# Writing out every engine's order by hand in a convolution and attention kernel: depthwise taps, Winograd transforms, reciprocals and a spread on ScalarE's queue

## The chip, the cores and the metric

The kernel runs on one core of a Trainium2 chip. The metric is the device time of one execution in microseconds (us). A profiled execution gives the trace; its own time stands beside its span (first to last instruction) below.

## The reference, cut to what matters

The input x is (8, 512, 32, 32) in float32. Two layers follow each other, each as x + layer(groupnorm(x)) with 32 groups of 16 channels.

```python
# layer 0: C = 256, two inner blocks, 4 heads of 64
t = silu(bn(conv1x1(gn(x), cv1_w)));  ys = [t[:, :256], t[:, 256:]]
for i in range(2):
    z = silu(bn(conv3x3(ys[-1], m_cv1_w[i])))
    q, k, v = split(conv1x1(z, m_qkv_w[i]))              # 4 heads, 1024 positions
    a = softmax(q @ (k + rw + rh) / 8);  z = a @ v
    ys.append(ys[-1] + silu(bn(conv1x1(z, m_cv2_w[i]))))
x = x + silu(bn(conv1x1(concat(ys), cv2_w)))             # 1024 -> 512 channels
# layer 1
h = prune(relu(bn(depthwise3x3(gn(x)) + dw_b)), 4.0)     # a channel whose maximum is under 4 becomes 0
x = x + prune(relu(bn(conv1x1(h, pw_w) + pw_b)), 0.001)
```

## The kernel before, in words

A run of `fast_kernel` does all the work; `general_kernel`, a slow form behind a flag, is not entered on these inputs. Channels lie on the 128 partitions, so an image is `KC` = 4 chunks of [128, 1024]. The outer loop is over the `B` = 8 images. For image b the stages are:

1. `cv1` (L398): the first 1x1 convolution. Output tiles m = 2, 3 go to `yp[0]`, m = 0, 1 are four half tiles `ps_y` into `y0`.
2. `conv3(0)` (L432): the 3x3 convolution in Winograd form. `along_rows(j)` and `across_rows(j)` (VectorE, with two narrow copies on ScalarE) make the transformed inputs in the idle tiles `kr`, `vt`, `qy` for j = 0, 1, 2; `products(j)` (L505) multiplies them with weights from the ring, twice for each j (m = 0, 1); `rows_back` copies one component with ScalarE (L517) and combines four with VectorE (L520 to L523); the closing step subtracts the outer plane (L555) and applies Silu (L557) to give `z[:, m]`.
3. `qkv(0)` (L567): `ps_qk` for k (VectorE adds one bias table at L591, GpSimd the other at L594), `ps_v` (copied at L608), `ps_qk` for q (copied at L612). All use the two PSUM buffers of `ps_big`.
4. `attention` (L615): 32 steps of two halves each. `scores(s)` makes `ps_s` (L633), ScalarE takes `Exp` into `e` (L641), VectorE adds up `sum` (L648); `values(s - 2)` accumulates `ps_av` (L657). TensorE runs one `scores` and one `values` in 1.72 us. When a half's 16 steps are done, `sums(m)` multiplies the sums with ones (`ps_dn`, L676), VectorE takes the reciprocal (L683), ScalarE copies `ps_dn` for a range check (L684), eight DMAs of 64 KB spread the reciprocals over the partitions into `rw` (L690), and `scale(m)` multiplies `z[:, m]` with them (L699). For m = 0 this happens in the middle of the loop (s = 20 to 28), for m = 1 after it.
5. `cv2m(0)` (L721): four tiles `ps_m`, each a k = 0 and a k = 1 matmul (k = 1 reads `z[:, 1]`), Silu, and an add into `yp[1]`.
6. `conv3(1)`, `qkv(1)`, `attention`, `cv2m(1)`: the second block.
7. `cv2` (L739): four output tiles of eight k steps (`ps_cv`, L757); `finish(m)` (L765) applies Silu on ScalarE (L159) and adds into `xt[m]` (L770).
8. Layer 1. `layer1_front` (L333): group norm statistics of `xt` (L303, L304), small matmuls `pm` and `pv` (L310, L318), `xn` and the middle tap on ScalarE (L324, L353), eight taps a chunk on VectorE (L350), Relu on ScalarE, a maximum (L359) and the pruning product on GpSimd (L361). `layer1_back` (L369): `ps_pw` half tiles (L377), Relu, maximum (L391), add into `xt` (L393), store. Layer 1 of image b fills holes of image b + 1: its pieces are closures in lists (`front`, `late`, `back`), and `pump(list, n)` emits the next n pieces at the place where it stands.

The order in the source is not the order on the engines: the tile framework's scheduler may move an instruction ahead of others on its engine when it holds that it is ready. `tc.issue_after` in `conv3` pins one group. Loads of x, the weight ring (`NRING` = 4 tiles of 1 MB) and stores go through SP's queue, in the scheduler's order.

Of the kernel before, what the change touches and what calls it, by code (L numbers as in the profile page):

```python
# [8 lines left out]
F32 = mybir.dt.float32  # L9
# [4 lines left out]
P = 128  # L14
# [15 lines left out]

@with_exitstack
def fast_kernel(
# [16 lines left out]
    nc = tc.nc  # L49
# [283 lines left out]
    def layer1_front():  # L333

        norm = {}

        def normed(c):
            norm[c] = work_tile("xn")
            return norm[c]

        gn = [group_norm(xt, normed, chunks) for chunks in ((0, 1), (2, 3))]
        work = [gn[0][0], None, gn[0][1], None, gn[0][2], None, gn[0][3], None]
        for c in range(KC):

            def tap(t, c=c):
                dst, src = img(ht[c]), img(norm[c])
                dy, dx = t // 3 - 1, t % 3 - 1
                o = dst[:, max(0, -dy) : F - max(0, dy), max(0, -dx) : F - max(0, dx)]
                i = src[:, max(0, dy) : F - max(0, -dy), max(0, dx) : F - max(0, -dx)]
                nc.vector.scalar_tensor_tensor(o, i, dw[:, c, t : t + 1], o, ALU.mult, ALU.add)  # L350

            def first(c=c):
                nc.scalar.mul(ht[c], norm[c], dw[:, c, 4:5])  # L353

            def last(c=c):
                norm.pop(c)
                act(ht[c], ht[c], AF.Relu, BN4 + c)
                keep = small.tile([P, 1], F32, tag="keep", name="keep")
                nc.vector.tensor_reduce(keep, ht[c], AX.X, ALU.max)  # L359
                nc.vector.tensor_scalar(keep, keep, 4.0, None, ALU.is_ge)  # L360
                nc.gpsimd.tensor_scalar(ht[c], ht[c], keep, 1.0, ALU.mult, ALU.mult)  # L361

            apply = gn[c // 2][4 + c % 2]
            work.append(lambda apply=apply, first=first: (apply(), first()))
            work += [lambda t=t, tap=tap: tap(t) for t in range(9) if t != 4]
            work.append(last)
        return work, gn[1][:4]

    def layer1_back(b):  # L369
# [4 lines left out]
        def half(m, n):  # L374
# [11 lines left out]
            w = box[m]  # L386
            act(w[:, n * 512 : (n + 1) * 512], ps, AF.Relu, BN5 + m)
            if n == 0:
                return
# [6 lines left out]
        return [lambda m=m, n=n: half(m, n) for m in range(KC) for n in range(2)]  # L396

    def cv1(stats, bg, per):  # L398

        for m in (2, 3):  # L400
            ps = big_tile("ps_cv1")
            for k in range(KC):
# [8 lines left out]
                if k == 1:  # L411
                    pump(stats)
            pump(stats)
            act(inner(yp[0], m - 2), by_phase(flat(ps)), AF.Silu, BN0 + m)
            pump(bg, per)
# [14 lines left out]
        return [lambda m=m, n=n: half(m, n) for m in range(2) for n in range(2)]  # L430

    def conv3(l, fill):  # L432
# [61 lines left out]
        def products(j):  # L494
# [4 lines left out]
            with Weights() as wt:  # L499
                u = wt.rearrange("p (i c k o) -> p i c k o", i=2, c=4, k=2)  # L500
                for c in (1, 2, 0, 3):
                    for i in range(2):
                        at = place[c] * 256 + i * P
                        for k in range(2):
                            keep["ins"] = nc.tensor.matmul(  # L505
# [19 lines left out]
        across_rows(0, along_rows(0))  # L525
        across_rows(1, along_rows(1))
        inner_planes = [work_tile("mid") for _ in range(2)]
        outer_planes = [work_tile("mid") for _ in range(2)]
        for m in range(2):
            rows_back(products(0), inner_planes[m][:, :512])  # L530
        across_rows(2, along_rows(2))
        ys = []
        for m in range(2):
            rows_back(products(1), inner_planes[m][:, 512:])
# [16 lines left out]
        for m in range(2):  # L551
            pc = outer_planes[m][:, :512]
            rows_back(products(2), pc)
# [10 lines left out]
        with tc.issue_after(keep["ins"].ins):  # L564
            pump(fill, len(fill))

    def qkv(l, bg, per):  # L567
        with Weights() as wt:
# [16 lines left out]

            for m, ps in enumerate(products((2, 3))):
# [28 lines left out]
    def attention(bg, every, tail):  # L615
# [85 lines left out]
        for s in range(len(steps) + 2):  # L701
# [4 lines left out]
            if s == 20:  # L706
                check = sums(0)
# [593 lines left out]
```

## Time and profile before

| what | value |
|---|---|
| median of 3 runs | 2950.03 us (2949.51 to 2951.57) |
| the profiled execution | 2950.13 us, span 2948.3 us, mean granted TensorE clock 0.974 |
| TensorE / VectorE / ScalarE / GpSimd busy | 91% / 66% / 39% / 6% of the span |
| one steady image | 354.9 us (ps_c of conv3(0) at 764.51 us to the same at 1119.37 us) |
| TensorE busy in that image | 331.9 us |
| VectorE, ScalarE busy in that image | 235.9 us, 142.2 us |
| chain that ended last | TensorE 55%, VectorE 23%, ScalarE 5% of the span |

How to read the rows in the next part: a timeline row gives the start and length in us, the engine (a "q" after it: its queue's issuing part), the line, the operation with output and inputs, the form, a count, and in brackets the idle time before it with what ended it. A matmul in float32 appears as two records. A window row gives the stretch, then the busy time of TensorE, its weight loads, VectorE, ScalarE and GpSimd, then the granted TensorE clock and the DMA engines' share and rate. In a row for a line, three durations are the least, the median and the greatest in ns.

### The profile page before, as it was taken

What the parts mean: (1) busy time and instruction counts of PE and PEld (TensorE: products, weight loads), DVE (VectorE), ACT (ScalarE), POOL (GpSimd) and SP (SyncE); (2) the same over time, 40 slices, a digit from 0 to 9 for tenths busy, and PEclk for the clock granted to TensorE, in tenths of its full rate; (3) what the DMA queues carried; (4) which work ended last, traced back from release to release, by engine and by line L of the source; (5) the groups of instructions that cost most, each with busy time, mean ns of one, the idle gap of its engine ahead of it and who ended that gap; (6) DMA issues with size and microseconds to landing.
All of it is one profiled execution on the core that took longest, in us unless ns stands there. A gap on an engine that the chain in (4) does not pass through costs nothing.

```text
span 2948.3 us, 36194 instructions
## 1 busy us (share of the span) xinstructions
PE 2676.8 (91%) x14946; PEld 1449.8 (49%) x14946; DVE 1932.4 (66%) x2513; ACT 1160.0 (39%) x1386; POOL 163.0 (6%) x97
## 2 busy tenths in 40 slices
PE   6879989999899998999999999999989999899984
PEld 4444454544646445464454545545454544545431
DVE  6765478753976639665596646975478753877536
ACT  3534335253352533524334342434325343352522
POOL 1000001000100001000010000100001000100001
PEclk9989999999999999999999999999999999999997
DMA  8510130311303013130131202221121301203000
GB/s 322 192 61 23 57 118 30 111 30 63 113 23 125 15 65 125 30 111 15 57 126 43 97 21 78 98 86 54 43 98 63 112 29 50 97 22 118 22 7 30
DMA packets 90333, 219.75 MB, mean 75 GB/s; under 512 B 8880, under 2 KB 54192, under 8 KB 77616
## 3 DMA queue, kind: packets, MB, share of 16 engines
q1 hardware_dynamic: 89728, 216.04, 21.5%
q8 instruction: 119, 1.95, 0.3%
q10 hardware_dynamic: 432, 1.32, 0.1%
q14 instruction: 54, 0.44, 0.0%
HBM read 171.19 MB, written 29.36 MB: 68 GB/s over the span
## 4 chain that ended last, share of the span: by engine, by line
PE 55%; DVE 23%; ACT 5%; issue 2%; SPq 1%; POOL 1%; DMA 0%; DVEq 0%; ACTq 0%; POOLq 0%
PE ps_cv L757 12%; PE ps_av L657 12%; PE ps_s L633 11%; DVE ht L350 10%; PE ps_c L505 8%; PE ps_pw L377 4%; PE ps_qk L577 3%; PE ps_m L726 3%; DVE r L683 2%; PE ps_v L601 2%; ACT e L641 1%; DVE kr L591 1%; SPq L690 1%; ACT c L159 1%; DVE keep L359 1%
## 5 line engine op out<-in xcount | busy, mean ns | idle before, releaser
L633 PE MATMUL ps_s<-qy,kr 64*64 64x512 f32 x4096 | 576.2, 595 | 79.9 <-ACT e L641 78.6
L641 ACT ACTIVATE e<-ps_s 128x1024 f32<-128x1024 f32 x512 | 520.1, 1024 | 269.0 <-PE ps_s L633 266.5
L657 PE MATMUL ps_av<-e,vt 64*64 64x512 f32 x4096 | 572.2, 593 | 0.0
L648 DVE TENSOR_TENSOR sum<-sum,e 128x1024 f32<-128x1024 f32 x384 | 471.8, 1229 | 152.2 <-ACT e L641 144.7
L633 PEld LDWEIGHTS ps_s<-qy,kr 64*64 64x64 f32 x4096 | 208.7, 133 | 330.0 <-ACT e L641 132.9
L657 PEld LDWEIGHTS ps_av<-e,vt 64*64 64x64 f32 x4096 | 225.4, 133 | 222.5 <-issue 145.0
L350 DVE SCALAR_TENSOR_TENSOR ht<-xn,v_sb,ht 128x961 f32<-128x961 f32 (+1 forms) x256 | 318.1, 1283 | 5.0 <-ACT ht L353 4.4
L377 PE MATMUL ps_pw<-ht,wpw_sb 128*128 128x512 f32 x512 | 230.8, 605 | 27.1 <-POOL ht L361 27.1
L757 PE MATMUL ps_cv<-yp,wring 128*128 128x512 f32 x512 | 230.4, 596 | 0.0
L577 PE MATMUL ps_qk<-z,wring 128*128 128x512 f32 x512 | 226.7, 596 | 2.8 <-ACT z L557 2.8
L645 DVE TENSOR_TENSOR sum<-e 128x1024 f32<-128x1024 f32 x64 | 78.2, 1221 | 199.1 <-ACT e L641 196.3
L505 PE MATMUL ps_c<-kr,wring 128*128 128x128 f32 x1024 | 138.8, 305 | 57.5 <-ACT kr L492 39.9
L377 PEld LDWEIGHTS ps_pw<-ht,wpw_sb 128*128 128x128 f32 x512 | 97.1, 193 | 153.9 <-issue 112.5
L505 PEld LDWEIGHTS ps_c<-kr,wring 128*128 128x128 f32 x1024 | 136.0, 220 | 70.5 <-ACT kr L492 45.5
L517 ACT COPY c<-ps_c 128x256 f32<-128x256 f32 x96 | 35.8, 373 | 331.5 <-PE ps_c L505 281.3
L577 PEld LDWEIGHTS ps_qk<-z,wring 128*128 128x128 f32 x512 | 97.8, 191 | 119.3 <-issue 113.5
L770 DVE TENSOR_TENSOR xt<-c,xt 128x1024 f32<-128x1024 f32 x32 | 39.2, 1226 | 176.0 <-ACT c L159 176.0
L757 PEld LDWEIGHTS ps_cv<-yp,wring 128*128 128x128 f32 x512 | 95.5, 190 | 118.2 <-issue 118.2
L594 POOL TENSOR_TENSOR kr<-kr,v_sb 128x1024 f32<-128x1024 f32 x32 | 75.0, 2357 | 1298.8 <-DVE kr L591 1225.6
L159 ACT ACTIVATE c<-ps_cv,bi,sc 128x1024 f32<-128x1024 f32 x32 | 69.7, 2178 | 194.4 <-PE ps_cv L757 194.4
L683 DVE RECIPROCAL r<-ps_dn 128x512 f32<-128x512 f32 x32 | 107.3, 3354 | 49.9 <-PE ps_dn L676 49.9
L726 PE MATMUL ps_m<-z,wm_sb 128*128 128x512 f32 x256 | 119.2, 604 | 20.4 <-DVE z L699 20.4
(167 smaller groups left out, 3152.8 us busy)
## 6 DMA issues: line engine op xcount, KB each, us to landing
wring<-u SPq DMA_DIRECT2D x96, 1024.0 KB, 4.8
pt<-in_x SPq DMA_DIRECT2D x32, 512.0 KB, 5.8
xt<-in_x SPq DMA_DIRECT2D x32, 512.0 KB, 3.5
rw<-r SPq DMA_DIRECT2D x256, 64.0 KB, 2.0
wring<-in_w SPq DMA_DIRECT2D x32, 512.0 KB, 4.2
out<-xt SPq DMA_DIRECT2D x32, 512.0 KB, 2.7
wring<-in_wqkv SPq DMA_DIRECT2D x16, 768.0 KB, 4.3
u<-ucomp SPq DMA_DIRECT2D x24, 256.0 KB, 2.8
```

Of the source, the lines that this page charges most:

```text
L159: nc.scalar.activation(o, i, func, bias=bi[:, n : n + 1], scale=sc[:, n : n + 1])
L350: nc.vector.scalar_tensor_tensor(o, i, dw[:, c, t : t + 1], o, ALU.mult, ALU.add)
L377: nc.tensor.matmul(ps, wpw_sb[:, k, m * P : (m + 1) * P], ht[k][:, n * 512 : (n + 1) * 512], start=(k == 0), stop=(k == KC - 1),)
L505: keep["ins"] = nc.tensor.matmul(flat(ps)[:, at : at + P], u[:, i, c, k, :], component(j, c)[:, (2 * i + k) * P : (2 * i + k + 1) * P], st ...
L577: nc.tensor.matmul(ps[:, n, :], w[:, k, m * P : (m + 1) * P], z[:, k, n * 512 : (n + 1) * 512], start=(k == 0), stop=(k == 1),)
L633: nc.tensor.matmul(ps[half(c), a, :], kr[half(a), m, j : j + HD], qy[half(a), m, ih * 512 : (ih + 1) * 512], start=True, stop=True,)
L641: nc.scalar.activation(flat(e), flat(ps), AF.Exp, scale=HD ** -0.5)
L648: nc.vector.tensor_tensor(t, t, flat(e), ALU.add)
L657: nc.tensor.matmul(accs[m, ih][r][half(a), :], vt[half(r), jt, h * HD : (h + 1) * HD], e[half(r), a, :], start=(jt == 0), stop=(jt == last),)
L683: nc.vector.reciprocal(r[:, :512], dn)
L726: nc.tensor.matmul(ps, wm2_sb[:, l, k, m * P : (m + 1) * P], z[:, k, n * 512 : (n + 1) * 512], start=(k == 0), stop=(k == 1),)
L757: nc.tensor.matmul(ps[:, n, :], w[:, k, :], rhs(k, n), start=(k == 0), stop=(k == 2 * KC - 1),)
```

## The change

A wrapper around TensorE, VectorE, ScalarE and SP makes each instruction depend (without a semaphore) on the one that was written before it for the same engine, so that the scheduler keeps the written order. GpSimd is left as it was. The order itself is then written out: which tap, statistic, transform or finishing step stands between which others. Besides that,

- the reciprocal is split into four pieces of 128 columns, in steps 20 to 23 for m = 0 (`sums` moves from step 20 to 19, the spread is at step 25, `scale` at 29), and the check copy of `ps_dn` is written ahead of them;
- the eight DMAs that spread the reciprocals are issued from ScalarE's queue instead of SP's;
- `layer1_back` is split into half tiles and `finish(m)`; `layer1_front` gives separate lists `early`, `late`, `before`, `taps`;
- in `conv3` the row transforms for j = 2 stand ahead of the first `rows_back`, and `along_back`, `close` and the fillers have fixed places;
- the second block's weight transform for image 0 is spread over `qkv(0)` (15 pieces) instead of standing ahead of the attention.

```diff
+class InOrder:
+    def __getattr__(self, name):
+        method = getattr(self.engine, name)
+        def call(*args, **kwargs):
+            made = method(*args, **kwargs)
+            if self.last is not None:
...
+                self.tc.add_manual_dep(made.ins, self.last, how, reason="in_order")
+            self.last = made.ins.name
+            return made
+        return call
+class Engines:
...
+        self.tensor, self.vector = InOrder(tc, nc.tensor), InOrder(tc, nc.vector)
+        self.scalar, self.sync = InOrder(tc, nc.scalar), InOrder(tc, nc.sync)
+        self.gpsimd = nc.gpsimd
...
-    nc = tc.nc
+    nc = Engines(tc)
# layer1_front
+        def before(c):
+            gn[c // 2][4 + c % 2]()
+            nc.scalar.mul(ht[c], norm[c], dw[:, c, 4:5])
...
+            taps += [lambda c=c, t=t: tap(c, t) for t in range(9) if t != 4]
+            taps[-1] = lambda c=c, last=taps[-1]: (last(), relu(c))
+            if c:
+                taps.insert(9 * c, lambda c=c: prune(c - 1))
+        taps.append(lambda: prune(KC - 1))
+        return gn[0][:4], gn[1][:4], [lambda c=c: before(c) for c in range(KC)], taps
# conv3
-        with tc.issue_after(keep["ins"].ins):
-            pump(fill, len(fill))
+        across_rows(0, along_rows(0))
+        pump(fill, early)
+        across_rows(1, along_rows(1))
+        pair = along_rows(2)
+        rows_back(products(0), inner_planes[0][:, :512])
+        across_rows(2, pair)
+        rows_back(products(0), inner_planes[1][:, :512])
+        rows_back(products(1), inner_planes[0][:, 512:])
+        along_back(0)
+        rows_back(products(1), inner_planes[1][:, 512:])
+        pump(ends_work)
+        along_back(1)
+        ms = products(2)
+        pump(ends_work)
+        close(0, ms)
+        ms = products(2)
+        flush(fill)
+        close(1, ms)
+        flush(ends_work)
# sums
-            nc.vector.reciprocal(r[:, :512], dn)
             nc.scalar.activation(r[:, 512:], dn, AF.Copy, accum_out=rng[:, n : n + 1])
+            def part(q):
+                c = slice(q * 128, (q + 1) * 128)
+                nc.vector.reciprocal(r[:, c], dn[:, c])
+            def spread():
...
-                    nc.sync.dma_start(
+                        nc.scalar.dma_start(
...
+            if s == 19:
+                parts, spread, check = sums(0)
+            if 20 <= s < 24:
+                parts[s - 20]()
+            if s == 25:
+                spread()
+                check()
+            if s == 29:
                 scale(0)
-            if s % every == every - 1:
+            if s in when:
                 pump(bg)
         flush(bg)
         tail[0]()
-        check = sums(1)
+        parts, spread, check = sums(1)
+        for part in parts:
+            part()
+        spread()
         tail[1]()
         scale(1)
         check()
# the loop over images
+        first, y0_work = cv1()
+        pump(first)
+        pump(taps, 2)
+        pump(late)
+        pump(first)
+        pump(taps, 2)
+        pump(late)
+        pump(before)
+        pump(first)
+        pump(taps, 2)
+        pump(before)
+        pump(first)
+        pump(taps, 3)
+        pump(y0_work, 2)
+        conv3(0, y0_work, 1, [])
...
+            taps = transform_weights(1)
+        elif b + 1 < B:
+            load(pt, b + 1)
+        qkv(0, taps, (4, 2, 2, 2, 2, 2, 2))
+        attention(taps, QUIET, (lambda: pump(halves), lambda: pump(halves, 2)))
+        pump(finishes)
...
         cv2m(0)
+        pump(halves, 2)
+        conv3(1, halves, 1, finishes)
         load(xt, b)
+        stats = group_norm(pt, lambda c: pt[c], range(KC)) if b + 1 < B else []
+        qkv(1, [], (0,) * 7)
         products, finish = cv2()
         attention(
             stats[:KC],
+            (6, 10, 14, 17),
+            (lambda: products(0, (0, 1)), lambda: (products(0, (2, 3, 4, 5)), products(1, (0,)))),
         )
...
+        early, late, before, taps = layer1_front()
+        products(1, (1, 2, 3))
...
+        products(2, (5, 6, 7))
+        pump(before)
         finish(2)
+        pump(taps, 3)
         pump(late)
+        products(3, (0, 1, 2, 3))
+        pump(taps, 3)
+        pump(before)
+        products(3, (4, 5, 6, 7))
+        pump(taps, 4)
         finish(3)
         pump(late)
+        halves, finishes = layer1_back(b)
```

## The prediction

> **What bounds the kernel now.** I read the page's busy times first, then TensorE's timeline over one steady image (764.5 to 1119.4 us), then the ScalarE and VectorE timelines beside each hole in it, and last the window table for the granted clock.
>
> ```profile
> PE 2676.8 (91%) x14946; PEld 1449.8 (49%) x14946; DVE 1932.4 (66%) x2513; ACT 1160.0 (39%) x1386; POOL 163.0 (6%) x97
> ```
>
> TensorE is busy 91% and the change alters none of its work, so only the other 271 us and the clock can move. These timeline rows start after the holes (in brackets: idle time, and who ended it):
>
> ```profile
> 764.51 9.47 PE L505 MATMUL ps_c<-kr,wring 128*128 128x128 f32 x64 [5.71 <-ACT kr L492]
> 824.68 1.09 PE L633 MATMUL ps_s<-qy,kr 64*64 64x512 f32 x8 [2.45 <-ACT e L641]
> 860.84 1.09 PE L633 MATMUL ps_s<-qy,kr 64*64 64x512 f32 x8 [1.91 <-ACT e L641]
> 894.43 4.56 PE L726 MATMUL ps_m<-z,wm_sb 128*128 128x512 f32 x10 [1.80 <-DVE z L699]
> 919.55 7.38 PE L505 MATMUL ps_c<-vt,wring 128*128 128x128 f32 x64 [2.35 <-issue]
> 1093.21 0.38 PE L310 MATMUL pm<-mv,g_sb 128*128 128x2 f32 x2 [0.81 <-DVE mv L304]
> ```
>
> With smaller ones (.98 before ps_v, .89 in conv3(0), 1.25 at each attention start, 1.91 in the second attention) an image has 23 us of holes. A hole can cost twice. The window table's columns are us, then busy time by engine, then granted clock:
>
> ```profile
> 764.50:768.90 4.40, 4.39 (x20) 4.40 (x21) 4.37 (x8) 0.34 (x2) 1.90 (x1) 0.50 0.00 0
> 563.80:567.40 3.60, 3.60 (x18) 3.60 (x19) 3.60 (x8) 0.00 (x0) 0.00 (x0) 0.54 0.94 366
> 919.60:923.20 3.60, 3.60 (x33) 3.60 (x34) 3.58 (x8) 0.00 (x0) 0.00 (x0) 1.00 0.93 387
> ```
>
> After the 5.7 us hole the clock is halved for 4.4 us (2.2 lost); after the 2.35 us hole at 563.8 for 3.4 (1.7 lost), after the same hole at 919.6 not at all. In conv3(1) three of seven such holes did it, the 5.7 ones always, holes up to 2.46 in attention never.
>
> **The change part by part.** I followed the instruction order of the changed program on each engine; TensorE's is nearly the old one.
>
> *Taps.* Before, VectorE runs 16 taps between the last cv2 tile and conv3(0), and TensorE waits for it.
>
> ```profile
> 738.84 5.80 DVE L350 SCALAR_TENSOR_TENSOR ht<-xn,v_sb,ht 128x961 f32<-128x961 f32 x5
> ```
>
> A tap is 1.14 us. The new order puts nine during products(3), where VectorE idles 10.9 us, and eight (9.1 us) after. Counted from the end of products(2): cv1's second tile ends at 31.1 on TensorE, its Silu, behind xn and ht of chunks 2 and 3, at 33.1, relu(1) and prune(1) at 35.5, four transform steps and the first kr (.6 each) at 38.6; TensorE has three y0 halves (10.3) until 41.4. Cover 2.8: hole 5.7 to 0, half clock gone, 7.9 us on each of images 1 to 7: −55.
>
> *Its price at pm.* ScalarE now does relu(0), behind eight taps, ahead of finish(3)'s Silu. From the same start: Silu 2.2, add 1.25, three taps 3.4, statistics 1.5, five taps 5.7, relu 1.25: 15.3, against 13.8 for products(3). Silu 2.2, add 1.25 and statistics 1.5 end at 20.3; TensorE, after four cv1 matmuls (3.4), is at pm at 17.2. The hole goes from .8 to some 3.2: +2.4, seven times: +17.
>
> *conv3(0) and qkv(0).* The last y0 Silu stands ahead of close(1)'s copy: from the end of that half on TensorE, Silu .8, copy .4, four combining steps 1.35, ends .6 and Silu 1.25 bring z[1] after 4.5, and the k=0 half of qk covers 3.4: 1.1. Four taps (4.6) stand ahead of the first kr add (1.84), which so begins as qk ends; both PSUM buffers are taken and ps_v waits 1.75, then .5 for the second add behind two taps. That is 3.35 instead of 2.05: +1.4 with the clock left alone, seven times: +10. At the attention's start relu(3) stands ahead of the Exp table load (1.25 to 3.15), but the 2.45 hole from a relu among the Exps goes: −.5, −4.
>
> *conv3(1).* The finish(m) work (2.55 us each) no longer sits between VectorE's vt operations: holes .5, 2.35, .18, .34 become about 1.05 (the same late copy, here behind two pw Silus): −2.3 seven times, −16, and the three half clocks −5.
>
> *Reciprocal and spread.* Before, the .6 us copy waits for the 3.36 us reciprocal, and the Exps behind both; SP issues the eight DMAs.
>
> ```profile
> 853.54 1.02 ACT L641 ACTIVATE e<-ps_s 128x1024 f32<-128x1024 f32 x1 [0.69 <-PE ps_s L633]
> 859.19 0.60 ACT L684 ACTIVATE r<-ps_dn 128x512 f32<-128x512 f32 x1 [4.62 <-DVE r L683]
> 859.77 1.02 ACT L641 ACTIVATE e<-ps_s 128x1024 f32<-128x1024 f32 x1
> ```
>
> An Exp 4.5 us late thus left a hole of 1.9 beside 1.0 of ps_dn matmuls: 1.6 is absorbed. Quarters hide the reciprocal: one takes .84 beside a sum of 1.14, step 1.72. But the DMAs now stand in ScalarE's own queue at s=25, with check() (.72) and every later Exp behind them. Their price:
>
> ```profile
> L690 SPq DMA_DIRECT2D rw<-r x256: 507/588/1764, 156.5 to 2814.5; - x128
> DMA to landing us min/median/max: 1.9/2.0/3.8
> 0.73 0.41 ACTq L92 DMA_DIRECT2D v_sb<-in_vecs  x1
> 1.66 0.45 ACTq L96 DMA_DIRECT2D w_sb<-in_w  x1
> ```
>
> No row has this transfer on ScalarE. It lies between .43 (its three loads) and .59 (the same transfer on SP) an issue; I take .59, the row with the same shape. Eight with the gaps between them are 5.0. ScalarE idles .7 between Exps, so the next is 5.0 + .7 − .7 = 5.0 late, hole 5.0 − 1.6 = 3.4 instead of 1.9: +1.5, sixteen times: +25. At .43 the eight are 3.6 and the sum is 1.4 less each time.
>
> [...]
>
> *Attention's ends.* The new reciprocal waits for ScalarE's copy (.7, and .3 for four pieces; 512 columns take .68 and 256 .41 in the transforms, so some .1 of an instruction is fixed), so z[1] comes 12.4 us after ps_dn instead of 11.4. Written order also gives cv2m one k=0 matmul before it needs z[1], where three ran before (.86 each). cv2m(0): cover 6.9+.86, hole 4.7 instead of 1.8. cv2m(1): ten cv2 matmuls (8.6) and one, hole about 3.0 to 3.3 instead of none. Together +5.9, eight times: +47. The pw Silus queued behind the spread finish before z[1] does.
>
> *The ends.* Image 0 has the second weight transform in qkv(0) instead of ahead of attention (hole 10.7): about −3. The last image has nine taps done early, but three pw matmuls fewer: −4. The moved pt, xt and ring loads and the pt statistics cost nothing: they land in steps that TensorE fills (30 us and more of cover; uncovered, a load's landing is 3 to 6 us).
>
> *The clock.* New holes above 3 us: pm and the attention start (7 each), mid-attention (16), cv2m (8 and 8). Between three in seven (2.35 us) and always (5.7) I take .65, for the 4.7 ones .9: 32 events. At 1.5 (1.7 less what lies in the hole): +48. Bounds: 0, and 46 at 1.7, +78.
>
> [...]
>
> Sum: −55+17+10−4+25+47−16−5−7+48 = +60. The profiled execution took 2950.1 us (span 2948.3), the runs' median 2950.0, so 3010.
>
> **The rivals.**
> 1. An issue on ScalarE costs what its three loads did (.43), or the clock mostly holds. Mid-attention and cv2m lose 1.4 less in 32 places (−45), and some 15 clock events go (−22): 2943. For it: the ACTq rows. Against: other shapes, and on SP 128-row loads are cheaper (.33) than rw.
> 2. The issue costs ScalarE under .1 us. The mid-attention holes vanish (3.4 × 16 = 54), those at cv2m shrink to 1.0 and 0 (55), 23 clock events go (34): 2867, clearly faster. It decides below about .45 an issue, where the sum crosses zero. No row is below .32.
> 3. VectorE is still last at conv3(0), since taps beside GpSimd's kr adds are slower (six took 8.6 us at 804): the 55 is not won, 3065.
>
> That the order isn't kept is no rival: the built program shows it.
>
> **How the numbers follow.** The forecast gets .63, rivals .2, .08 and .09. Within .2% (about what a measurement of this kernel can tell from no change) is 2944 to 2956. The forecast's own range, clock from none to all, is 2962 to 3040: slower. Rival 1 splits: .12 faster, .05 same, .03 slower. Faster .12+.08 = .20, same .05, slower .75. The range takes in rival 1 and most of rival 3, leaving out rival 2 and some of each tail: 2922 to 3060.
>
> **What the changed profile would show.** All operations will carry the wrapper's one line, so rows go by tiles. Right: ScalarE's queue rows for rw of .55 or more in groups of eight, a hole near 3.4 before ps_s in mid-attention, 4 to 5 before ps_m in cv2m(0), about 3 in cv2m(1) and at pm, none before ps_c<-kr, and PEclk .50 stretches behind some of them. Wrong: rw issues near .1, cv2m holes under 2, a hole still before conv3(0), or these holes with the clock at 1.00.

## The result, and the profile after

The changed kernel takes 3090.43 us (median of four runs, 3087.06 to 3092.15) against 2949.77 for the kernel before: ratio 1.0474, interval 1.0456 to 1.0492. It is slower, as forecast, but by 141 us and not by 60, and outside the stated range (2922 to 3060). The profiled execution has a span of 3085.3 us against 2948.3: 137.0 to explain.

The page of the changed kernel, busy times and the chain that ended last:

```profile
PE 2745.5 (89%) x14946; PEld 1411.1 (46%) x14946; DVE 1975.7 (64%) x2609; ACT 1166.1 (38%) x1386; POOL 157.7 (5%) x97
PE 64%; DVE 21%; ACT 6%; ACTq 4%; DMA 2%; issue 2%; POOL 0%; DVEq 0%; SPq 0%; POOLq 0%
```

TensorE has the same 14,946 matmul records and is busy 68.7 us longer, while its mean granted clock fell from 0.974 to 0.951, with stretches at half clock (0.50 in the window rows below). Its idle time grew by 68.3 (span less busy). So one half of the loss is holes (idle time of TensorE), the other half clock. ScalarE's queue (ACTq), 0% of the chain before, now carries 4% of it.

TensorE's timeline, one image (770.2 to 1142.7 us, 372.5 long; 354.9 before). Each row stands behind a hole, which is in brackets with what ended it:

```profile
770.16 0.59 PE L41 MATMUL pm<-mv,g_sb 128*128 128x2 f32 x2 [4.34 <-DVE mv L41]
...
830.28 3.72 PE L41 MATMUL ps_v<-wring,z 128*128 128x256 f32 x16 [1.83 <-DVE kr L41]
836.11 1.38 PE L41 MATMUL ps_v<-wring,z 128*128 128x256 f32 x4 [2.10 <-DVE kr L41]
...
854.52 1.99 PE L41 MATMUL ps_s<-qy,kr 64*64 64x512 f32 x8 [3.95 <-ACT e L41]
...
905.63 1.13 PE L41 MATMUL ps_s<-qy,kr 64*64 64x512 f32 x4 [3.33 <-ACT e L41]
...
932.76 2.07 PE L41 MATMUL ps_m<-z,wm_sb 128*128 128x512 f32 x2 [4.35 <-DVE z L41]
...
1055.94 1.13 PE L41 MATMUL ps_s<-qy,kr 64*64 64x512 f32 x4 [4.31 <-ACT e L41]
...
1083.20 1.22 PE L41 MATMUL ps_m<-z,wm_sb 128*128 128x512 f32 x1 [2.83 <-DVE z L41]
```

The hole before `ps_c<-kr` is gone, as forecast; mid-attention and cv2m are where the forecast put them. Not forecast at this size: the two ps_v holes, the 3.95 at the attention's start, and pm's 4.34. The window table (us, busy time by engine, granted clock) behind three of these holes and behind one of the next image:

```profile
836.90:840.20 3.30, 3.30 (x9) 2.64 (x8) 3.30 (x3) 2.14 (x2) 2.11 (x1) 0.50 0.00 0
854.60:857.30 2.70, 2.70 (x16) 0.88 (x20) 1.23 (x1) 1.45 (x2) 0.00 (x0) 0.50 0.03 6
905.70:908.50 2.80, 2.80 (x16) 0.97 (x20) 2.36 (x2) 1.55 (x2) 0.00 (x0) 0.50 0.01 3
1429.40:1432.80 3.40, 3.40 (x32) 1.21 (x36) 3.19 (x3) 2.35 (x3) 0.00 (x0) 1.00 0.00 0
```

The last row is an exception (one of two among 33 holes above 3 us): a hole of 3.33 with the clock left whole. ScalarE issues rw at the price that was assumed (median .603 against .59):

```profile
L41 ACTq DMA_DIRECT2D rw<-r x256: 514/603/1389, 168.4 to 2942.4; - x128
```

Forecast and measurement by stage, cut at the first matmul of each (the first pm of an image stands in cv2), clock included, over the whole program (us):

| stages | forecast | measured |
|---|---|---|
| pm to the end of conv3(0) (taps, pm, clock) | -31 | -31 |
| qkv(0) | +10 | +56 |
| both attentions, to the first ps_m | +43 | +63 |
| cv2m(0), cv2m(1) | +66 | +60 |
| conv3(1), qkv(1) | -21 | -21 |
| start of the program and last image's end | -7 | +10 |
| sum | +60 | +137 |

Two cv2 matmuls an image (1.72 us) run in the second attention in the changed kernel and behind the first pm in the kernel before. Without this shift of work the first row is -19, the attentions +49, cv2m +63 and the ends +8.

### The profile page after: what moved, and what is told of

The parts are those of the page before. It is cut to its first block, busy times and chain, and to the rows that moved or that the text cites. A ratio compares the mean times of both kernels' runs of the same rounds, so it can differ in the third digit from the quotient of the medians.

```text
span 3085.3 us, 36329 instructions
## 1 busy us (share of the span) xinstructions
PE 2745.5 (89%) x14946; PEld 1411.1 (46%) x14946; DVE 1975.7 (64%) x2609; ACT 1166.1 (38%) x1386; POOL 157.7 (5%) x97
## 4 chain that ended last, share of the span: by engine, by line
PE 64%; DVE 21%; ACT 6%; ACTq 4%; DMA 2%; issue 2%; POOL 0%; DVEq 0%; SPq 0%; POOLq 0%
PE ps_av L41 14%; PE ps_s L41 13%; PE ps_cv L41 12%; DVE ht L41 8%; PE ps_c L41 8%; PE ps_m L41 4%; PE ps_pw L41 4%; ACTq L41 4%; PE ps_y L41 3%; PE ps_qk L41 3%; DMA rw<-r 2%; PE ps_v L41 2%; DVE r L41 2%; DVE mid L41 2%; DVE kr L41 2%
## 5 line engine op out<-in xcount | busy, mean ns | idle before, releaser
L41 PE MATMUL ps_s<-qy,kr 64*64 64x512 f32 x4096 | 579.1, 615 | 98.3 <-ACT e L41 96.8
L41 ACT ACTIVATE e<-ps_s 128x1024 f32<-128x1024 f32 x512 | 520.7, 1023 | 316.1 <-PE ps_s L41 315.9
L41 DVE TENSOR_TENSOR sum<-sum,e 128x1024 f32<-128x1024 f32 x384 | 470.6, 1225 | 208.1 <-ACT e L41 200.5
L41 PE MATMUL ps_av<-e,vt 64*64 64x512 f32 x4096 | 569.4, 607 | 0.0
L41 PEld LDWEIGHTS ps_s<-qy,kr 64*64 64x64 f32 x4096 | 191.9, 137 | 376.9 <-issue 175.3
L41 DVE SCALAR_TENSOR_TENSOR ht<-xn,v_sb,ht 128x961 f32<-128x961 f32 (+1 forms) x256 | 342.5, 1345 | 5.8
L41 PEld LDWEIGHTS ps_av<-e,vt 64*64 64x64 f32 x4096 | 201.9, 137 | 264.1 <-issue 212.7
L41 PE MATMUL ps_pw<-ht,wpw_sb 128*128 128x512 f32 x512 | 232.7, 608 | 32.6 <-POOL ht L394 32.6
L41 PE MATMUL ps_qk<-z,wring 128*128 128x512 f32 x512 | 232.5, 598 | 18.0 <-DVE mid L41 14.3
L41 PE MATMUL ps_cv<-yp,wring 128*128 128x512 f32 x512 | 231.1, 597 | 0.0
L41 DVE TENSOR_TENSOR sum<-e 128x1024 f32<-128x1024 f32 x64 | 78.4, 1225 | 228.2 <-ACT e L41 228.2
L41 PE MATMUL ps_m<-z,wm_sb 128*128 128x512 f32 x256 | 143.3, 712 | 62.1 <-DVE z L41 62.1
L41 PEld LDWEIGHTS ps_pw<-ht,wpw_sb 128*128 128x128 f32 x512 | 97.0, 194 | 161.3 <-issue 115.7
L41 PE MATMUL ps_v<-wring,z 128*128 128x256 f32 x512 | 130.5, 416 | 36.6 <-DVE kr L41 36.6
L41 PEld LDWEIGHTS ps_qk<-z,wring 128*128 128x128 f32 x512 | 94.4, 190 | 143.5 <-issue 122.1
L41 DVE RECIPROCAL r<-ps_dn 128x128 f32<-128x128 f32 x128 | 114.8, 928 | 61.4 <-ACT r L41 61.4
L41 PEld LDWEIGHTS ps_cv<-yp,wring 128*128 128x128 f32 x512 | 94.9, 190 | 114.3 <-issue 114.3
L41 PEld LDWEIGHTS ps_v<-wring,z 128*128 128x128 f32 x512 | 104.9, 209 | 69.0 <-DVE kr L41 52.9
L41 PE MATMUL ps_cv<-pt,w_sb 128*128 128x512 f32 x256 | 132.5, 674 | 2.8 <-ACT pt L41 2.8
L41 PE MATMUL ps_c<-kr,wring 128*128 128x128 f32 x1024 | 121.5, 281 | 14.8 <-DMA wring<-u 9.7
L41 PEld LDWEIGHTS ps_c<-kr,wring 128*128 128x128 f32 x1024 | 121.1, 198 | 23.1 <-ACT vt L41 10.5
```

The source lines that it names most:

```text
L41: made = method(*args, **kwargs)
```

## The experiments

All times are medians. The letter E and a number name a run; "changed" is the changed kernel at 3090. Each run carried a fresh time of the kernel before (2949.7 to 2950.9).

| run | what | us | ratio to before |
|---|---|---|---|
| E1 | changed, spread on SP | 3005.8 | 1.0192 (1.0175 to 1.0209) |
| E2 | changed, no taps between VectorE's kr adds | 3085.0 | 1.0459 (1.0442 to 1.0477) |
| E3 | changed, three items behind finish(3) | 3100.1 | 1.0505 (1.0487 to 1.0522) |
| E4 | changed, second spread on two queues | 3034.6 | 1.0283 (1.0266 to 1.0300) |
| E5 | E2, and three items into the attention | 3033.0 | 1.0278 (1.0261 to 1.0295) |
| E6 | E3's items behind pv | 3091.7 | 1.0480 (1.0462 to 1.0497) |
| E7 | before, spread on ScalarE | 3061.3 | 1.0379 (1.0361 to 1.0396) |
| E8 | changed without the wrapper | 2872.7 | 0.9733 (0.9717 to 0.9749) |
| E9 | wrapper on TensorE alone | 3039.3 | 1.0297 (1.0279 to 1.0316) |
| E10 | wrapper on ScalarE alone | 2936.9 | 0.9957 (0.9942 to 0.9972) |
| E11 | wrapper on VectorE alone | 2943.1 | 0.9974 (0.9965 to 0.9984) |
| E12 | E8, spreads on SP and on both queues | 2803.8 | 0.9505 (0.9488 to 0.9522) |
| E13 | changed, pm and pv later | 3089.4 | 1.0469 (1.0450 to 1.0488) |
| E14 | changed, three k = 0 matmuls ahead | 3043.2 | 1.0313 (1.0295 to 1.0331) |
| E15 | written order, all places mended | 2855.4 | 0.9679 (0.9662 to 0.9696) |
| E16 | E15's source (less pm, k = 0) without the wrapper | 2802.0 | 0.9495 (0.9478 to 0.9512) |
| E17 | E15, two more moves on ScalarE | 2827.8 | 0.9584 (0.9568 to 0.9600) |

### The spread: E1, E4, E7

E1, one word in `spread()`:

```diff
-                        nc.scalar.dma_start(
+                        nc.sync.dma_start(
```

> The changed kernel with the eight spreading DMAs on SP's queue again. Theory: at mid-attention it is the eight issues (5.0 us) in ScalarE's own queue that hold the next Exp; with them on SP only the check copy (.63) is left ahead of it, so the holes of 3.33 and 4.31 before ps_s fall to 0 to .5 and the half-clock windows behind them go: about 10 us an image, 75 to 80 in all, some 3010 us (2995 to 3030). The cv2m holes stay at 4.35 and 2.83, since SP issues at the same pitch (.633 before) and the order of the steps is unchanged. Rival: the mid-attention holes come from the new order around the reciprocal (copy first, four pieces, the check waiting for r); then they stay at 1.9 or more and the time falls by under 25 us.

Measured: 3005.8, 85 less than changed. The mid-attention holes are gone, cv2m keeps 4.4 and 2.6. ScalarE's timeline at mid-attention, first of the changed kernel, then of E1:

```profile
898.88 5.01 ACTq L41 DMA_DIRECT2D rw<-r  x8
903.95 0.63 ACT L41 ACTIVATE r<-r 128x512 f32<-128x512 f32 x1 [4.50 <-DMA rw<-r]
904.48 0.19 ACT L41 ACTIVATION_READ_ACCUMULATOR r<-r 128x1 f32 x1
904.57 1.92 ACT L41 ACTIVATE e<-ps_s 128x1024 f32<-128x1024 f32 x2
```

```profile
884.61 0.58 ACT L41 COPY part<-ps_av 128x512 f32<-128x512 f32 x1
885.07 0.64 ACT L41 ACTIVATE r<-r 128x512 f32<-128x512 f32 x1
885.60 0.20 ACT L41 ACTIVATION_READ_ACCUMULATOR r<-r 128x1 f32 x1
885.70 1.02 ACT L41 ACTIVATE e<-ps_s 128x1024 f32<-128x1024 f32 x1
```

Two Exps come back to back at 904.57 after 5.7 us of DMA issues and check; with the issues on SP an Exp follows the check at once.

E4 sends the second spread's DMAs alternately:

```diff
-                        nc.scalar.dma_start(
+                        q = nc.scalar if m == 0 else (nc.sync, nc.scalar)[h]
+                        q.dma_start(
```

> The changed kernel with the eight DMAs of the second half's spread (the one after the attention loop) issued in turn from SP and ScalarE, four each; the first half's stay on ScalarE. Theory: at cv2m the chain copy, four reciprocals, eight issues one after the other, landing, scale sets z[1]; two queues issue in 2.5 us instead of 5.0, so the holes 4.35 and 2.83 fall to about 1.9 and .4, and the half clocks behind them go: 2.45 + 1.7 (less where a window had fallen into the hole), twice an image, 55 to 66 us in all, some 3030 us (3020 to 3045). Rival: the landing takes longer when two queues issue at once, or one queue's issue price rises, so that the holes shrink by under 1 us: 3070 to 3090.

Measured: 3034.6, 56 less. cv2m(0) 4.35 to 2.2, cv2m(1) 2.83 to .5. ScalarE and SP, side by side:

```profile
1279.79 2.44 ACTq L41 DMA_DIRECT2D rw<-r  x4
1279.86 2.67 SPq L41 DMA_DIRECT2D rw<-r  x4
```

The two queues issue at once here, four in 2.44 and four in 2.67, where the eight on ScalarE's took 5.01; the median landing stays 2.0.

E7 puts the spread on ScalarE in the kernel before, nothing else:

> The kernel before with one change: the eight spreading DMAs issued from ScalarE's queue. Nothing else, no written order. Theory: the eight issues (5.0 us) stand ahead of the next Exps, behind the whole reciprocal, and nothing absorbs them: the mid-attention hole grows from 1.9 to about 6.9, with a half-clock window behind it (1.7 or more), 16 times: +105 us, 3055 us (3035 to 3075); the holes at cv2m stay as they are, since the issue pitch is the same. Rival: the issues overlap with the wait for the reciprocal or with VectorE's sums, and the spread is worth no more than the +25 of the forecast: 2965 to 2985.

Measured: 3061.3, 112 more than before. TensorE's hole there grew from 1.91 to 6.55:

```profile
1253.89 0.51 ACTq L690 DMA_DIRECT2D rw<-r  x1
1254.28 0.19 ACT L684 ACTIVATION_READ_ACCUMULATOR r<-ps_dn 128x1 f32 x1
1254.44 4.46 ACTq L690 DMA_DIRECT2D rw<-r  x7
1259.01 1.94 ACT L641 ACTIVATE e<-ps_s 128x1024 f32<-128x1024 f32 x2 [4.54 <-DMA rw<-r]
```

So the other queue is a loss in either order. That it is smaller in the changed kernel fits that its pieces hide the reciprocal, which no run tests by itself.

### qkv(0): E2, E5

> The changed kernel with the taps of qkv(0) counted (3, 0, 0, 4, 4, 3, 2) instead of (4, 2, 2, 2, 2, 2, 2): none between or behind the two kr adds. Theory: the two taps between the kr adds run beside GpSimd's add at 2.0 us each, not 1.14, and TensorE waits for the second kr add; without them the holes 1.83 and 2.10 before ps_v fall to about .4 each or less, the half clock behind them goes, and the last tap ends about 3 us sooner, so that the Relu ahead of the Exps no longer holds them: the hole at the attention's start falls from 3.95 to 1.25. Per image 3.1 + 1.7 and 2.7 + 1.7, seven times: 60 us, some 3030 (3015 to 3050). Rival: the taps only carry their price to a later place (the Relu in front of the Exps comes no sooner, the start hole stays near 4 or grows): 3060 to 3090.

```diff
-        qkv(0, taps, (4, 2, 2, 2, 2, 2, 2))
+        qkv(0, taps, (3, 0, 0, 4, 4, 3, 2))
```

Measured: 3085.0, 5 less: the rival. Both halves of the reason show in TensorE's timeline of E2:

```profile
1202.06 1.13 PE L41 MATMUL ps_v<-wring,z 128*128 128x256 f32 x4 [0.57 <-DVE kr L41]
...
1226.46 1.13 PE L41 MATMUL ps_s<-qy,kr 64*64 64x512 f32 x4 [7.78 <-ACT e L41]
```

The ps_v holes shrank from 3.93 to .57, and all of it came back before the Exps, which stand behind the last Relu. ScalarE, VectorE and GpSimd in E2:

```profile
1222.83 1.24 ACT L41 ACTIVATE ht<-ht,bi,sc 128x1024 f32<-128x1024 f32 x1 [5.30 <-DVE ht L41]
1224.09 1.28 ACT L41 ACT_TABLE_LOAD   x1
1203.83 7.86 DVE L41 SCALAR_TENSOR_TENSOR ht<-xn,v_sb,ht 128x992 f32<-128x992 f32 x5
1202.15 4.85 POOL L653 TENSOR_TENSOR kr<-kr,v_sb 128x1024 f32<-128x1024 f32 x2 [39.44 <-DVE kr L41]
```

The five taps behind VectorE's second add still run beside GpSimd's adds (until 1207.0) and take 7.86; so E2, and E5 below with the same counts there, take the taps out from between VectorE's two adds but not from beside GpSimd's, against what their expectations say. VectorE and GpSimd in the changed kernel show why the holes were there:

```profile
828.33 1.90 DVE L41 TENSOR_TENSOR kr<-ps_qk,v_sb 128x1024 f32<-128x1024 f32 x1
830.15 4.07 DVE L41 SCALAR_TENSOR_TENSOR ht<-xn,v_sb,ht 128x961 f32<-128x961 f32 x2
834.15 1.90 DVE L41 TENSOR_TENSOR kr<-ps_qk,v_sb 128x1024 f32<-128x1024 f32 x1
835.99 4.03 DVE L41 SCALAR_TENSOR_TENSOR ht<-xn,v_sb,ht 128x961 f32<-128x961 f32 x2
830.38 2.80 POOL L653 TENSOR_TENSOR kr<-kr,v_sb 128x1024 f32<-128x1024 f32 x1 [40.70 <-DVE kr L41]
```

The two taps between the adds take 4.07, not the forecast 2.3. One row for the four taps from 830.2 to 840.0 (least, median, greatest ns) tells how:

```profile
L41 DVE SCALAR_TENSOR_TENSOR ht<-xn,v_sb,ht x4: 1179/2018/2919, 830.2 to 837.1; 128x961 f32<-128x961 f32 x3, 128x992 f32<-128x992 f32 x1
```

In each pair the first tap (1.18 and 1.19) starts ahead of GpSimd's add; the second takes 2.8 to 2.9 and ends 1.04 after that add (830.38 + 2.80 = 833.18, and 834.22). E5 takes the same kernel and lets the attention's fixed places have the last three items:

```diff
-        qkv(0, taps, (4, 2, 2, 2, 2, 2, 2))
+        qkv(0, taps, (3, 0, 0, 4, 4, 2, 0))
```

> The changed kernel with the taps of qkv(0) counted (3, 0, 0, 4, 4, 2, 0): none beside GpSimd's kr adds, and the last two taps of chunk 3 with their Relu, as well as its pruning, in the attention's fixed places (steps 5, 8, 11). Theory: in the run that only moved the taps off the kr adds, the start hole grew to 7.8 because VectorE's remaining 12 pieces end no sooner than before and the Exps stand behind the last Relu on ScalarE. With three pieces fewer the Relu no longer stands ahead of the Exps: the start hole falls from 3.95 to 1.25, the two ps_v holes to about .6 together, and the half clocks of both places go: 3.3 + 1.7 + 2.7 + 2.2 = 9.9 an image, seven times some 70 us: 3020 us (3010 to 3040), less what the Relu costs among the Exps (0 to 1 an image). Rival: the Relu among the Exps costs a hole of its own of 2 to 4 (the kernel before had 2.45 there): 3040 to 3065.

Measured: 3033.0, 57 less than changed. ps_v .61, start 1.31, and one new hole of 1.42 where the Relu stands among the Exps: inside the expected span.

### The place of pm: E3, E6, E13

E3 and E6 move the four items ahead of `finish(3)`, keeping one there; E3 puts the other three right behind its statistics, E6 further on:

```diff
-        pump(taps, 4)
+        pump(taps, 1)
         finish(3)
         pump(late)
+        pump(taps, 3)          # E3 only; E6: counts 1, 2, 4, 5 in cv1
```

> The changed kernel with three of the four items (last tap of chunk 0 with its Relu, a tap of chunk 1, prune(0)) that stand ahead of finish(3) put behind the group norm statistics that follow it. Theory: the hole of 4.35 before pm is the Relu of chunk 0 ahead of finish(3)'s Silu on ScalarE (2.2 us) and the taps it waits for; with them behind, the hole falls to about 1.5 to 2.2, and the half-clock window there (6.8 us, some 2 net of the hole) goes in most images: 4 to 5 us, seven times, some 3058 us (3050 to 3070). Rival: VectorE then idles while it waits for the Silu and comes late to conv3(0): a new hole of 2 or 3 before ps_c<-kr, no gain (3080 to 3095).

> The changed kernel with three items less on VectorE ahead of finish(3) (as in the run before) and these three now behind the second small matmul pv, in the later places of cv1 (counts 1, 2, 4, 5 instead of 2, 2, 2, 3). Theory: the run before moved the same items, the pm hole fell to 1.67 as expected and the new hole of 1.99 before pv came from their standing ahead of the copy of pm; behind pv they hold nobody: pm hole 1.7, no pv hole, half clock there mostly gone: 4.3 an image, seven times, 3060 us (3050 to 3072). Rival: VectorE comes late at conv3(0) by the 3.4 us of the three items: a hole of 1 to 3 before ps_c<-kr, 3080 to 3095.

Measured: 3100.1 and 3091.7. In both the pm hole fell to 1.67, and nothing was won. E3 made a hole of 1.99 before pv (its three items stand ahead of the copy of pm). In E6 it came back as 2.88 before `ps_c<-vt` instead of .91 and, in six of seven images, 5.6 at the attention's start instead of 3.95: the rival in time, though not at the place that it named (`ps_c<-kr`). E13 leaves VectorE and ScalarE as written and gives TensorE four more matmuls to do ahead of pm and pv:

```diff
         pump(first)
         pump(taps, 2)
+        pump(first)
         pump(late)
+        pump(taps, 2)
         pump(first)
-        pump(taps, 2)
         pump(late)
         pump(before)
-        pump(first)
```

> The changed kernel, wrapper and all, with pm written four cv1 matmuls later on TensorE, and pv four later as well; all else in its place. Theory: TensorE's written order costs so much because it can't run the cv1 matmuls that are ready while pm waits for the statistics (the free order runs pm behind them, hole .94). With four of them ahead of it (3.4 us) the hole of 4.35 falls to about .9 and its half-clock window goes (3.4, of which some 2 outside the hole): 5 to 6 an image, seven times some 38 us: 3052 us (3045 to 3062). Rival: the second tile's Silu, and with it conv3(0), waits for what pv releases, and the hole only moves: 3075 or more.

Measured: 3089.4. TensorE's timeline:

```profile
1148.07 0.38 PE L41 MATMUL pm<-mv,g_sb 128*128 128x2 f32 x2 [0.92 <-DVE mv L41]
...
1167.11 7.38 PE L41 MATMUL ps_c<-kr,wring 128*128 128x128 f32 x64 [1.16 <-ACT kr L41]
1177.58 0.77 PE L41 MATMUL ps_c<-vt,wring 128*128 128x128 f32 x2 [3.08 <-ACT c L41]
```

The hole of 4.35 fell to .92 as expected, and 1.16 and 3.08 (instead of .91) stand in conv3(0): the rival (3075 or more). In six of seven images the hole in front of the Exps is 5.64 instead of 3.95, too. The mean granted clock of the run is 0.952, against 0.951 in the changed kernel. Three ways to shrink the pm hole, three times no gain: it was slack of TensorE in a stretch, from cv2's last tile to the first Exp, whose end other engines set. That these are ScalarE's and VectorE's written orders is argued here; E17 tests ScalarE's.

### The wrapper: E8 to E11

E8 is the changed kernel with `nc = tc.nc` for `nc = Engines(tc)`; in E9, E10 and E11 one engine alone is wrapped.

> The changed kernel without the wrapper: the same source order, but the scheduler may move instructions as in the kernel before. The spread stays on ScalarE. Theory: the loss lies in the spread and in the fixed places that were badly chosen (taps beside the kr adds, Relu ahead of the Silu, one k = 0 matmul ahead of z[1]); the scheduler undoes the latter but not the spread, so that it lands between the run with the spread on SP's queue and the changed kernel, some 3045 us (3020 to 3075). Rival: the scheduler moves the taps and the reciprocal pieces to worse places than the written ones: 3090 or more.

> The changed kernel with the wrapper on TensorE alone; ScalarE, VectorE and SP are left to the scheduler. The whole wrapper costs 3090 - 2873 = 217 us. Theory: TensorE's written order costs only the missing k = 0 matmuls at cv2m (the free order has three there and no hole at cv2m(1), stage 4.5 us shorter; cv2m(0) 1.6 shorter), eight times some 50 us: 2920 us (2900 to 2945). Rival: the TensorE order is where most of the loss lies (matmuls can't fill a hole any more): 2980 or more.

> The changed kernel with the wrapper on ScalarE alone. Theory: the holes of the stages that grew most are each released by ScalarE behind an operation that waits for something else: the Relu of chunk 0 ahead of finish(3)'s Silu (pm hole 4.35), the check copy behind the spread ahead of the Exps (1.7 more than in the free order, twice an image), the last Relu ahead of the table load and the Exps: 3 + 1.7 with the half clock, 3.4, 2 to 3: some 10 to 11 an image, 80 us: 2950 us (2920 to 2985). Rival: with VectorE free to feed it in the right order, ScalarE's written order costs little: under 2900.

> The changed kernel with the wrapper on VectorE alone. Theory: the two taps between the kr adds (qkv(0), 5.4 us an image longer than free, half clock counted) and the late last tap are VectorE's share, with some of the pm hole (ten taps ahead of the add): 7 to 9 an image, 60 us: 2930 us (2905 to 2965). The three single wrappers then add up to about the 217. Rival: it takes the orders of two engines together to make a wait (one in front of the wrong operation, the other unable to pass it), so that each alone costs under 30.

Measured: 2872.7 for E8, under every expectation: without the wrapper the same source, with its spread still on ScalarE, beats the kernel before by 2.7%. The page's busy line of E8 has TensorE at 93% of a span of 2871.1, and its idle time is 196.7 instead of 339.8:

```profile
PE 2674.4 (93%) x14946; PEld 1381.4 (48%) x14946; DVE 1917.3 (67%) x2609; ACT 1164.7 (41%) x1386; POOL 153.4 (5%) x97
```

Against E8, TensorE's order alone costs 167 (E9, where its rival held), ScalarE's 64, VectorE's 70. They add up to 301, more than the 218 of all together, so they share waits; SP's order alone was not run. E10 and E11 lie within their ranges, but not by the theories given. With ScalarE alone in written order pm's hole is 1.09, not 4.35, and the loss against E8 stands in qkv(0) (23 us), qkv(1) (15), cv2m(0) (12) and the attentions (18). With VectorE alone the largest part, 41, is conv3(1) with qkv(1), with a hole of 3.33 before the latter's first `ps_qk`, which the theory does not name. TensorE around pm, first E9, then E8:

```profile
1122.10 3.60 PE L41 MATMUL ps_cv<-pt,w_sb 128*128 128x512 f32 x8
1130.92 0.58 PE L41 MATMUL pm<-mv,g_sb 128*128 128x2 f32 x2 [5.22 <-DVE mv L336]
```

```profile
1070.71 7.89 PE L447 MATMUL ps_cv<-pt,w_sb 128*128 128x512 f32 x18
1079.54 0.38 PE L340 MATMUL pm<-mv,g_sb 128*128 128x2 f32 x2 [0.94 <-DVE mv L334]
```

In E9 four cv1 matmuls (8 records) run and then pm holds everything behind it for 5.22 us; in E8 the scheduler has moved nine ahead of it. By stages E9 loses against E8, an image: 7.2 from pm to conv3(0), 6.0 in conv3(1), 4.4 in cv2m(1) and 2.6 in cv2m(0), about 1.7 in each attention.

### Mending: E12, E14 to E17

E12 and E16 have no wrapper; the first spread goes to SP, the second alternately to both queues (E4's edit with `nc.sync` for m = 0). E14 writes three k = 0 matmuls ahead in `cv2m`. E15 puts E1, E4, E5, E13 and E14 together, with `close(1, ms)` ahead of `flush(fill)`; E17 moves on from E15:

```diff
         pump(taps, 2)
-        pump(before)
         pump(first)
         pump(taps, 3)
+        pump(before)
...
+        if l:
+            flush(fill)
         close(1, ms)
         flush(fill)
```

> The changed kernel without the wrapper, with the first half's spread on SP's queue and the second half's issued in turn from SP and ScalarE. Theory: as in the ordered kernel (85 us for the one, 56 for the other), but from smaller holes: mid-attention 1.64 and 1.72 go to 0 to .3, the half clocks in the attentions go, cv2m(0) falls from 2.8 to about .4: 1.5 + 1.5 + 2.4 + some 2 of clock, eight times: 50 to 60 us, 2815 us (2800 to 2840). Rival: the scheduler, which now sees the DMAs on another queue, places other work there and the gain is under 25.

> The changed kernel, wrapper and all, with the k = 0 matmuls of the first three cv2m tiles written ahead of the first k = 1. Theory: two more matmuls of .86 cover the wait for z[1]: cv2m(0) 4.35 to 2.6, cv2m(1) 2.83 to 1.1, and the half clock behind the second goes: 1.7 + 1.7 + 1.7, eight times some 40 us: 3050 us (3040 to 3065). Rival: in cv2m(0) the banks of the extra tiles are held by the pw Relus, which stand behind the eight issues on ScalarE, so that only cv2m(1) gains: 27 us, 3063 and over.

> The changed kernel, all in written order, with every place mended that the runs have pointed to: first spread on SP, second in turn from SP and ScalarE, qkv(0)'s counts (3, 0, 0, 4, 4, 2, 0), pm and pv four matmuls later, three k = 0 matmuls ahead, and close(1) written ahead of the last fillers (its copy no longer behind a y0 Silu, two holes of .95 an image). Theory: the loss is the sum of these places and not the wrapper as such: 85 + 56 + 57 + 38 + 30 (what is left for the k = 0 matmuls beside the split) + 15: 2810 us (2790 to 2830), as fast as the free order with the same spread (2804). Rival: a written order can't follow the times that differ from image to image, or the mended places share one wait: 2840 or more.

> The free order with the same spread (the run at 2804), qkv(0)'s counts (3, 0, 0, 4, 4, 2, 0) and close(1) written ahead of the fillers. Theory: the scheduler already passes what isn't ready, so source places matter little to it: within 10 us of 2804; at best the hole of 2.00 before ps_qk goes (1.4 an image with the clock: 2780 to 2790). Rival: the scheduler puts the taps that are no longer in qkv(0) among the Exps, with holes of 1 to 2 there: 2810 to 2825.

> The written order with all places mended (2855), with two more moves on ScalarE: in cv1 the xn and middle tap of chunk 3 stand behind the second tile's Silu and the following taps, not ahead of them, and close(1) stands ahead of the fillers in conv3(0) only. Theory: what still separates it from the free order in a steady image is ScalarE's order in front of conv3(0): Silu and Relu wait 2.4 us behind xn and ht of chunk 3, so that VectorE idles 2.2 before prune(1) and comes late: holes of 1.16 and 3.08 before ps_c with a half clock. With 2.4 less they fall to 0 and about 1, and the hole of 2.20 in qkv(1) to 1.3 in all: 3.5 + 1 an image, seven times 32 us: 2823 us (2810 to 2838). Rival: the stretch is bound by VectorE's own work (taps and transforms), not by ScalarE's order, and the hole only moves back: 2848 or more.

Measured: E12 2803.8, as expected. E14 3043.2, as expected: the same two matmuls that the free order found by itself are worth 47. In cv2m(0) its rival shows as well: the second k = 0 matmul waits 2.23 for a Relu of pw (`[2.23 <-ACT pw L41]`), and the wait for z[1] behind it is only .17. E15 2855.4 missed its range; it is its rival's number. Its sum had 38 for pm, which E13 did not win. Its steady image is 342.8, against 338.0 in E12, with E13's 1.16 and 3.08 in conv3(0) left and a hole of 2.20 in qkv(1) (.95 and .34 in the changed kernel) that came with its early close(1); the first image's start and the last image's end take 17 more. ScalarE in E15 ahead of conv3(0):

```profile
1068.93 1.23 ACT L41 ACTIVATE xn<-xt,nb,rs 128x1024 f32<-128x1024 f32 x1
1070.19 1.15 ACT L41 ACTIVATE ht<-xn,v_sb 128x1024 f32<-128x1024 f32 x1
1071.24 1.19 ACT L41 ACTIVATE yp<-ps_cv,bi,sc 128x1024 f32<-128x1024 f32 x1
```

E16 2802.0: the free order gains nothing from source places that are worth 57 in the written one. E17 2827.8, as expected in sum: a steady image is 3.9 shorter than in E15, 1.0 of it in qkv(1). The hole before `ps_c<-kr` is gone; the next is 2.45, less than the 3.08 of E15, though not the 1 that was expected:

```profile
1080.95 1.24 PE L41 MATMUL ps_c<-vt,wring 128*128 128x128 f32 x9 [2.45 <-ACT c L41]
```

So in E13 and E15 it was ScalarE's order, two operations of chunk 3 ahead of the Silu that conv3(0) needs, that carried about half of what had come back there: E17's other move, close(1), touches conv3(1) alone. Its steady image is 338.9 against 337.8 in E16: in the steady images the written order with all these places mended comes nearly level with the free one. Of the 26 us between them, 17.5 lie at the two ends, mostly in the last image's tail (110.4 from the first pm of its layer 1 on, 96.2 in E16). That part was seen, not tested.

## Why the prediction was wrong, by its own steps

The direction and the places of the large holes were right; the sizes were not. Of the 77 us between forecast and measurement (60 and 137), 41 are TensorE's clock (busy time +28 forecast, +69 measured) and 36 are holes (+32 and +68). Two steps failed: the clock, priced at 32 events, and qkv(0), where two taps beside GpSimd's add were counted at 2.3 us and took 4.07.

- **Taps before conv3(0), pm**: the -31 agrees by chance; without the work that moved to the attention it is -19. The hole of 5.7 and its half clock went, as forecast. pm's hole was 4.34, not 3.2, with a half-clock window of 6.83 us at the end of each one in the steady images (the trace's clock records). From products(2) on, the eight taps ahead of the Relu took 10.0 instead of 9.1 (one starts 1.25 behind the last, not 1.14), and the add 1.73 instead of 1.25, beside GpSimd's pruning product:

```profile
757.15 7.41 DVE L41 SCALAR_TENSOR_TENSOR ht<-xn,v_sb,ht 128x992 f32<-128x992 f32 x6
766.81 1.73 DVE L41 TENSOR_TENSOR xt<-c,xt 128x1024 f32<-128x1024 f32 x1 [0.66 <-ACT c L41]
766.35 1.12 POOL L394 TENSOR_SCALAR ht<-ht,keep 128x1024 f32<-128x1024 f32 x1 [21.92 <-DVE keep L41]
```

- **conv3(0)/qkv(0)**: the stage that failed most, +10 forecast (3.35 less 2.05 is 1.30, so +9), +56 measured. "1.75, then .5 for the second add behind two taps" measured 1.83 and 2.10: the two taps took 4.07, not 2.3. The row for it was in the profile of before and in the prediction's third rival (six taps in 8.6 beside the adds, 1.8 more than six of 1.14), but it was used at conv3(0), where GpSimd does no add, and not at qkv(0), where the price belongs. The holes of this stage are 4.88 an image with the .95 before `ps_qk`, not 3.35: 11 of the 46 us. A half clock of 3.41 us follows the ps_v holes (1.7 lost an image, 12 in all), where the forecast left the clock alone. 12 more are image 0's weight transforms: with 4 given back in its attention they cost 8, where the forecast had -3. Most of the rest is a hole of .91 in conv3(0) from the transforms ahead of `rows_back`: the forecast took the old holes there (.89 and .18) for gone and counted that gain in this term.
- **Attention's start**: forecast -4 in all with a clock event. The Relu does stand ahead of the table load, but it comes 2.6 us after the first scores, since VectorE's last tap ends only then (850.9): hole 3.95. E5 moved the last items away and had 1.31.
- **Mid-attention**: hole 3.33 against 3.4 forecast, issue .60 against .59. Right, and E1 shows it to be the spread. In three halves it is 3.7, in one 4.31. The clock price was too low: of the 33 holes above 3 us between 400 and 2800 us, 31 have a half-clock window at their end in the trace's clock records, where the forecast counted .65 for most.
- **cv2m**: 4.35 and 2.83 against 4.7 and 3.0 to 3.3, +60 against +66. E4 and E14 confirm both causes, the issue time and the missing k = 0 matmuls.
- **conv3(1)**: -21, as forecast, though 4 of it are image 0's, which the term did not count.
- **Ends**: -7 forecast, +10 measured. The program starts its first matmul 3 us later, and the last image's pieces, all written one behind the other, end 7 us later.
- **The clock**: the forecast took 32 new events at 1.5, and gave back 20. TensorE's busy time, which holds the clock, grew by 69 instead of 28: nearly every hole above 3 us had its window (31 of 33), and so had each pair of ps_v holes and each cv2m(1) hole of 2.5 to 2.8 in the steady images (3.41 us each).
- **The rivals**: the issue price decided as forecast (.60). None of them asked what the fixed order itself costs: the prediction treated the wrapper as the means by which places are fixed and priced only the places. E8 shows that it costs 218, and that placing and splitting without it would have been a gain of 77 in spite of the spread.

E1 and E7 price the spread on ScalarE's queue at 85 and 112 us of the program: at mid-attention of the changed kernel the eight issues took 5.01 us, with a median landing of 2.0, and the check and the next Exps stood behind them.

## What to carry to other kernels

Before writing an engine's order by hand, list for each place where the engine will stand in front of a wait which ready instructions are behind it: a free order runs them, a written one can't, and here TensorE's queue was the dearest to get wrong (pm, the k = 0 matmuls). Here eight DMAs of 64 KB that followed each other held ScalarE's queue for 5.01 us (median .60 an issue); with them on SP's the program took 85 us less, and with the second spread on both queues 56 less. So try such a group on the queue of an engine with nothing to do, or on two. When a hole is removed and the time stays, follow the stretch to its next fixed point: here three edits that shrank the same hole moved it to pv, conv3(0) and the Exps, and part of it was won only when ScalarE's order in front of conv3(0) was changed.

## What the runs showed that was not expected

- In E4 the two queues issued at the same time, four in 2.44 and four in 2.67, where eight took 5.01 on one, and the median landing was 2.0 as in both kernels. That the price lies in the queue and not in the DMA engines is the author's reading of these numbers.
- In qkv(0) of the changed kernel the VectorE taps that came up during GpSimd's adds took up to 2.92, where the median of all taps is 1.24, and the add 2.80, where the least of its 32 is 1.96.
- The two ps_v holes, 1.83 and 2.10 with 3.7 us of work between them, are followed by a half-clock window of 3.41 us in the steady images, though holes up to 2.48 in the attention of the kernel before never were.
